# Layer 0's last five pairs of row tiles turned in 32x32 blocks by VectorE and moved through DRAM instead of transposed by TensorE

## The chip, the cores and the metric

The kernel runs on one NeuronCore of one Trainium2 chip. A core has a matrix engine (TensorE, PE in the profile, with PEld for its weight loads), a vector engine (VectorE, DVE), an engine for activation functions and copies (ScalarE, ACT), a general one (GpSimd, POOL) and a queue engine (SyncE, SP); the engines run side by side, each through its own instructions in order, and wait for one another by semaphores. Matrix results land in PSUM, everything else lies in SBUF, and transfers to and from DRAM are done by 16 DMA engines, started here by SP and by ACT. The metric is the device time of one execution in microseconds (us); lower is better.

## The reference, cut to what matters

There are N = 4096 nodes with D = 512 features and a dense 4096 x 4096 array `adj`. Layer 0 is attention inside 32 graphs of 128 nodes each, where the softmax's denominator runs over the whole row of `adj`; layer 1 is a graph attention with 8 heads over the mask `adj > 0`.

```python
h = jnp.maximum(_layernorm(x, axis=-1), 0.0)
# layer 0: attention within each graph of 128 nodes
query, key, value = h @ Wq.T + bq, h @ Wk.T + bk, h @ Wv.T + bv
a = jnp.where(mask, query @ key.T * scale, 0.0)
scores = (a + adj + adj) * jnp.where(mask, 1.0, -1000000.0)
x = x + (jax.nn.softmax(scores, axis=-1) * mask) @ value
# layer 1: 8 heads, one mask
h = jnp.maximum(_layernorm(x, axis=-1), 0.0)
mx = jnp.einsum('nf,hfd->hnd', h, W)
logits = s_i[:, :, None] + t_j[:, None, :]
attn = jax.nn.softmax(jnp.where(adj[None] > 0, logits, neg_inf), axis=-1)
x = x + einsum('hij,hjd->hid', attn, mx), heads side by side
```

## The kernel before, in words

**Tiles.** The 4096 rows are 32 row tiles of 128 (`NT`), one for each graph. Layer 0 takes two at a time: 16 pairs (`NG`, pair g is tiles 2g and 2g+1). A row of `adj` is read in two halves of 2048 columns (`load_adj`, 1 MB each, 7 buffers in turn), so a pair needs four.

**Stages.** A start (`fold`, up to about 42 us) multiplies the query and key weights into one matrix `m_sb` and works out what the biases add: `bk`, `bq` and a column `u_col` are spread into rows, `spread_bias` (L187) and L231, by matmuls of a broadcast column with the identity. Then comes layer 0's loop over g (42 to 335 us), then the last pair (to 349), then layer 1's projection for the tiles that are not yet projected (to 434), and layer 1's aggregation over the mask (`product`, L318 to L322, to the end).

**The loop over pairs.** Everything is written out by hand there (`tc.manual_schedule` for all five engines): each engine does its instructions in the order in which the program names them. In iteration g the names stand in this order:

- `load_pair(g + 2)` fetches the input rows of the pair two ahead into `xg`.
- `scores` (L578) multiplies this pair's queries gT with hT; VectorE adds twice the diagonal block of `adj` (L583), ScalarE takes the exponent.
- `queries` (L504) makes gT of pair g+1 in four PSUM groups, copied by ScalarE (L508). Between the groups, `mask_half` (VectorE, L144) writes the 8-bit mask of two row tiles of `adj` and `sum_half` (ScalarE, L547) sums the exponents of the same half; its elementwise output goes to `junk`, which nobody reads. `store_mask` writes the mask to `a_d` (L556), and `sum_half` starts the next `load_adj` into the half that it has done with (L110).
- `turned` transposes the attention weights (L601).
- `moments` and `normed0` (L117 to L129) normalise pair g+2: VectorE's statistics, GpSimd's inverse root, VectorE's normalisation.
- In iterations 7, 8, 9, 10 and 13, `prepare` (L271) projects a tile for layer 1 on PE.
- `values` (L517) makes v of pair g+1, `attend` (L609, L612) multiplies weights with v and adds the input; the sum x1 is stored to DRAM by ScalarE's queue (L615, `x_d<-x` in the profile). The row of tile g is fetched back (`fetch`, L439).
- `row_terms` (L491) is a dot product of each row of pair g+2 with `u_sb`.
- `turn` (L415) turns one tile of layer 1's normalised input in 32x32 blocks on VectorE; every four tiles `store` writes them to DRAM, and `move` (four transfers, L426 to L428) reads them back so that the whole is transposed: block (q, a) lands at (a, q).
- `turned0` transposes pair g+2 on PE: `relu_T`, four 128x128 transposes for a tile (L135), and one ScalarE relu from PSUM to `hT` (L136).

PSUM has four buffers `pp` for queries, projections, values and attend, used in turn. In layer 1's projection loop, the tile that is `far` = 10 tiles ahead decides when `move` is started: at `far % BY == 1`, with BY = 4.

The rule for the single transfer is that the place in the order decides: SP issues its transfers in the program's order, and one that has to wait holds those behind it.

Of the kernel before, what the change touches and what calls it, by code (L numbers as in the profile page):

```python
# [9 lines left out]
F32 = mybir.dt.float32  # L10
# [10 lines left out]
P = 128  # L21
N = 4096
D = 512
# [20 lines left out]
AB = 7  # L44
AHEAD = 10
# [8 lines left out]
def kernel(  # L54
# [33 lines left out]
    hT_d = dram.tile([NW, P, P // B, KC * P], F32, name="hT_d")  # L88
    x1_d = dram.tile([NT, P, D], F32, name="x1_d")
# [84 lines left out]
    def fold(sb, tmp, work, ps_t, ps_p, loads, between):  # L174
# [9 lines left out]
        def spread_bias(b):  # L184
            pp = ps_p.tile([P, D], F32, name="pp")
            for k in range(KC):
                nc.tensor.matmul(  # L187
                    pp[:, ts(k, P)], b[:, k : k + 1].to_broadcast([P, P]), ident,
                    start=True, stop=True,
                )  # L190
            row = work.tile([P, D], F32, name="b_row", tag="hn")
            nc.scalar.copy(row, pp)
            return row
# [33 lines left out]
        for m in range(KC):  # L227
            if m == 2:
                pp = ps_p.tile([P, D], F32, name="pp")
                for k in range(KC):  # L230
                    nc.tensor.matmul(  # L231
                        pp[:, ts(k, P)], u_col[:, k : k + 1].to_broadcast([P, P]), ident,
                        start=True, stop=True,
                    )
                nc.scalar.copy(u_sb, pp)
                pp = ps_p.tile([P, D], F32, name="pp")
                nc.tensor.matmul(pp[:, :1], zp.to_broadcast([P, P]), one, start=True, stop=True)
                nc.scalar.copy(z_sb, pp[:, :1])
            between(m, 0)
            pp = ps_p.tile([P, D], F32, name="pp")  # L240
            for k in range(KC):
                nc.tensor.matmul(  # L242
                    pp, wq[:, k, ts(m, P)], wk[:, k, :], start=(k == 0), stop=(k == KC - 1)
                )
            between(m, 1)
            nc.scalar.mul(m_sb[:, m, :], pp, SCALE)
# [140 lines left out]
    with ExitStack() as straight:  # L387
# [4 lines left out]
        with ExitStack() as prep:  # L392
# [71 lines left out]
            with (  # L464
# [20 lines left out]

                def row_terms(hns):

                    r = sb.tile([P, G], F32, name="r", bufs=3)
# [25 lines left out]
                def values(hT, t, later=False):  # L514
# [5 lines left out]
                    v = sb.tile([P, D], F32, name="v", bufs=4)  # L520
# [12 lines left out]
                def sum_half(i, h, diag, sums, counts):  # L533
# [9 lines left out]
                    for c0, c1 in pieces:  # L543
                        if c0 < c1:
                            n = counts[-1]
                            junk = sb.tile([P, NH], BF16, name="junk", bufs=1)
                            nc.scalar.activation(  # L547
                                junk[:, c0:c1], a[:, c0:c1], AF.Exp, scale=2.0 * NEG,
# [49 lines left out]
                def turned(s):  # L598
# [3 lines left out]
                    sT = sb.tile([P, G, P], F32, name="sT", bufs=1)  # L602
# [14 lines left out]
                def load_pair(g):  # L617
                    xg[g] = sb.tile([P, G, D], F32, name="xg", bufs=3)
# [44 lines left out]
                )  # L663
                for g in range(NG - 1):
                    new = G * (g + 1)
                    mine = g - 1
                    if g + 2 < NG:
                        load_pair(g + 2)
                    if g in (5, 9, 13):
                        store(g // BY - 1)  # L670
# [3 lines left out]
                    if g == NG - 2:  # L674
# [3 lines left out]
                        more = sb.tile([P, G, D], F32, name="xg", bufs=3)  # L678
# [19 lines left out]
                    s = scores(hT, gT, rs[g], *look)  # L698
                    ngT = queries(nhT, between)
                    sT = turned(s)  # L700
                    if g + 2 < NG:
                        ofs = [moments(xg[g + 2][:, t, :]) for t in range(G)]
# [10 lines left out]
                    if g + 2 < NG:  # L713
                        hns = normed0(g + 2, ofs)
# [12 lines left out]
                    if g + 2 < NG:  # L727
                        rs[g + 2] = row_terms(hns)
# [8 lines left out]
                    if g + 2 < NG:  # L737
                        nhT, hns = turned0(g + 2, hns)

# [37 lines left out]
            with by_hand:  # L777
# [6 lines left out]
                for i in range(LO, NT):  # L784
# [3 lines left out]
                    if far % BY == 1 and LO + AHEAD < far <= NT + 1:  # L788
# [414 lines left out]
```

## Time and profile before

| what | value |
|---|---|
| time, median of 3 runs | 931.07 us (929.63 to 931.77) |
| profiled execution | 930.15 us, span 928.3 us |
| TensorE busy | 919.4 us, 99% of the span |
| VectorE busy | 474.3 us, 51% |
| ScalarE busy | 261.1 us, 28% |
| GpSimd busy | 160.8 us, 17% |
| moved by DMA | 165.01 MB, mean 178 GB/s |
| `a<-adj`, issue to landing, median | 8.4 us for 1 MB |
| `mw<-a_d`, the same | 3.9 us for 128 KB |
| `x_d<-x`, the same | 7.3 us for 256 KB |

The page gives for each engine its busy time and its share of the span. A group of instructions is shown as line, engine, operation, output<-input, shape and count, then busy time and mean duration of one, then the idle time of the engine just before them and what ended it. Matmuls overlap in the array, so that a mean duration is longer than what one more of them costs; the chain of waits, which gives the time that a run of them took, shows the cost. The 40 slices show that the transfers are dense in the first third, where layer 0 reads `adj`, and thin afterwards:

```profile
DMA  8999999999899766762212122222222131313111
GB/s 333 415 333 390 366 372 377 345 368 352 309 350 370 238 203 182 208 154 57 69 52 85 55 83 61 76 69 68 82 56 83 55 91 46 91 46 92 46 46 37
```

A slice is 23.2 us. Layer 0's iterations start at 41.65 and then every 18.4 us, or every 21.9 where `prepare` is in them; iterations 9 to 14 start at 215.07, 236.95, 258.83, 277.20, 295.58 and 317.46.

### The profile page before, as it was taken

The numbers are of one execution on the slowest core, as the hardware profiler recorded it, in microseconds if no ns is written. First come the engines' busy times: TensorE is split into PE (matmuls) and PEld (weight loads), VectorE is DVE, ScalarE is ACT, GpSimd is POOL, SyncE is SP. The second block draws the span as 40 slices with busy tenths as digits, with TensorE's granted clock in tenths as the row PEclk, the third lists the DMA queues.
The fourth block names the chain that finished last, engine by engine and source line by source line (L and its number), as shares of the span: only waits on it lengthen the run. The fifth ranks groups of instructions, "written<-read, shape, count | busy, mean of one in ns | idle before, by whom it ended". The sixth has DMA issues, their size and how long they took to land.

```text
span 928.3 us, 13021 instructions
## 1 busy us (share of the span) xinstructions
PE 919.4 (99%) x4933; PEld 803.4 (87%) x4933; DVE 474.3 (51%) x1016; ACT 261.1 (28%) x507; POOL 160.8 (17%) x344
## 2 busy tenths in 40 slices
PE   9999999999999999999999999999999999999997
PEld 6776676767767778889999999999999999999997
DVE  4577987677778776736272424232333323242412
ACT  5477667655566653321000000000000000000000
POOL 1112111132211225644010101010101010101010
PEclk9999999999999999999999999999999999999999
DMA  8999999999899766762212122222222131313111
GB/s 333 415 333 390 366 372 377 345 368 352 309 350 370 238 203 182 208 154 57 69 52 85 55 83 61 76 69 68 82 56 83 55 91 46 91 46 92 46 46 37
DMA packets 63941, 165.01 MB, mean 178 GB/s; under 512 B 7042, under 2 KB 23810, under 8 KB 54658
## 3 DMA queue, kind: packets, MB, share of 16 engines
q1 hardware_dynamic: 54370, 147.35, 47.4%
q10 hardware_dynamic: 9504, 16.78, 4.8%
q8 instruction: 40, 0.66, 0.3%
q14 instruction: 27, 0.22, 0.1%
HBM read 122.16 MB, written 41.94 MB: 177 GB/s over the span
## 4 chain that ended last, share of the span: by engine, by line
PE 90%; DMA 6%; DVE 1%; ACT 1%; POOL 1%; issue 0%; SPq 0%; DVEq 0%; ACTq 0%
PE pg L322 52%; PE pp L517 10%; PE pp L504 10%; PE pp L271 9%; PE pss L578 3%; PE pp L609 3%; DMA xg<-x 2%; PE pp L242 1%; DMA row<-x_d 1%; PE pt L135 1%; DMA x_d<-x 1%; PE pl L322 1%; DMA a<-adj 1%; DMA hT_d<-blocks 0%; DMA bk_sb<-bk 0%
## 5 line engine op out<-in xcount | busy, mean ns | idle before, releaser
L322 PE MATMUL pg<-part,ata 128*128 128x348 f32 (+1 forms) x1536 | 246.8, 321 | 0.0
L322 PEld LDWEIGHTS pg<-part,ata 128*128 128x128 f32 x1536 | 244.5, 188 | 0.1
L322 PE MATMUL pg<-part,atb 128*128 128x348 f32 x1472 | 236.8, 322 | 0.0
L322 PEld LDWEIGHTS pg<-part,atb 128*128 128x128 f32 x1472 | 234.6, 189 | 0.1
L336 ACT COPY tot<-pg 128x522 f32<-128x522 f32 x31 | 18.5, 597 | 454.0 <-PE pg L322 454.0
L547 ACT ACTIVATE junk<-a 128x2048 bf16<-128x2048 f32 (+15 forms) x92 | 124.5, 1353 | 1.3
L517 PE MATMUL pp<-wv,hT 128*128 128x512 f32 x256 | 114.9, 592 | 0.0
L308 DVE CAST atb<-at 128x4096 fp32r<-128x4096 fp8e4 x16 | 36.7, 2295 | 152.6 <-PE pg L322 152.6
L271 PE MATMUL pp<-w1x,hT 128*128 128x256 f32 (+1 forms) x512 | 114.1, 383 | 0.3 <-DVE e L280 0.3
L504 PE MATMUL pp<-hT,m_sb 128*128 128x256 f32 x512 | 113.2, 379 | 0.0
L271 PEld LDWEIGHTS pp<-w1x,hT 128*128 128x128 f32 x512 | 96.7, 190 | 16.2 <-issue 1.9
L308 DVE CAST ata<-at 128x4096 fp32r<-128x4096 fp8e4 (+1 forms) x17 | 36.9, 2168 | 140.5 <-PE pg L322 140.4
L504 PEld LDWEIGHTS pp<-hT,m_sb 128*128 128x128 f32 x512 | 96.2, 190 | 12.8 <-issue 0.5
L517 PEld LDWEIGHTS pp<-wv,hT 128*128 128x128 f32 x256 | 47.9, 190 | 54.3 <-issue 53.5
L144 DVE TENSOR_SCALAR a<-a 128x512 fp8e4<-128x512 f32 x256 | 90.4, 447 | 1.3 <-DMA a<-adj 1.3
L854 POOL COPY den_all<-tot 128x1 f32<-128x1 f32 x31 | 5.7, 184 | 365.9 <-DVE tot L337 365.9
L858 POOL TENSOR_TENSOR tot<-tot,row 128x512 f32<-128x512 f32 x31 | 39.9, 1287 | 61.9 <-DVE tot L342 59.9
L121 POOL TENSOR_SCALAR ve<-mv 128x1 f32<-128x1 f32 x64 | 15.1, 236 | 190.4 <-DVE mv L119 190.3
L255 POOL TENSOR_TENSOR part<-e,part 128x522 fp32r<-128x522 f32 x32 | 40.7, 1271 | 12.8 <-ACT part L252 12.8
L123 POOL TENSOR_TENSOR rstd<-ve,neghalf 128x1 f32<-128x1 f32 x64 | 41.1, 642 | 5.3
L299 DVE STREAM_TRANSPOSE at<-mw 128x1024 f32<-128x1024 f32 x32 | 39.6, 1237 | 0.0
L280 DVE TENSOR_TENSOR e<-pp,e 128x256 f32<-128x256 f32 x64 | 25.1, 411 | 27.0 <-PE pp L271 13.7
(114 smaller groups left out, 658.4 us busy)
## 6 DMA issues: line engine op xcount, KB each, us to landing
a<-adj SPq DMA_DIRECT2D x64, 1024.0 KB, 8.4
a_d<-a SPq DMA_DIRECT2D x32, 512.0 KB, 9.0
mw<-a_d SPq DMA_DIRECT2D x128, 128.0 KB, 3.9
row<-x_d SPq DMA_DIRECT2D x60, 256.0 KB, 3.7
xg<-x SPq DMA_DIRECT2D x16, 512.0 KB, 10.7
x_d<-x ACTq DMA_DIRECT2D x32, 256.0 KB, 7.3
hT_d<-blocks SPq DMA_DIRECT2D x8, 1024.0 KB, 4.8
hT<-hT_d SPq DMA_DIRECT2D x32, 256.0 KB, 6.2
```

The source lines that it names most:

```text
L123: nc.gpsimd.tensor_tensor(rstd, ve, neghalf, ALU.pow)
L144: nc.vector.tensor_scalar(a8v[:, u], av[:, u], 0.0, None, ALU.is_gt, saturate=False)
L255: nc.gpsimd.tensor_sub(dst[:, :, 1, :], e3, dst[:, :, 0, :].bitcast(F32))
L271: nc.tensor.matmul(pm[g][:, :n], hT[:, k, :], w1x[:, k, g * HW : g * HW + n], start=(k == 0), stop=(k == KC - 1),)
L299: nc.vector.transpose(at8.rearrange("p c n b -> p (c n b)").bitcast(F32).rearrange("p (c u n) -> p c u n", c=NW, n=B), mw.rearrange("p u ( ...
L308: nc.vector.tensor_copy(at[:, c0 * BY : c1 * BY].rearrange("p (c b) q -> p c b q", b=BY), at8[:, c0:c1].rearrange("p c q b -> p c b q"),)
L322: nc.tensor.matmul(pg[:, : 2 * CW1].rearrange("p (s w) -> p s w", s=2)[:, :, :n], at[:, j, :], part(j)[:, c, :, :n], start=(j == 0), stop= ...
L504: nc.tensor.matmul(pp[:, : G * P], m_sb[:, k, ts(m, P)], hT[:, k, :], start=(k == 0), stop=(k == KC - 1),)
L517: nc.tensor.matmul(pp, hT[:, k, ts(t, P)], wv[:, k, :], start=(k == 0), stop=(k == KC - 1))
L547: nc.scalar.activation(junk[:, c0:c1], a[:, c0:c1], AF.Exp, scale=2.0 * NEG, accum_out=sums[:, n : n + 1],)
L578: nc.tensor.matmul(pss[:, t, :], gT[:, k, ts(t, P)], hT[:, k, ts(t, P)], start=(k == 0), stop=(k == KC - 1),)
L858: nc.gpsimd.tensor_add(num, num, row)
```

## The change

Pairs 11 to 15 of layer 0 (`BLOCKS = 11`) are no longer transposed by TensorE. `turn0` turns a normalised pair in 32x32 blocks on VectorE into a buffer `b0`; `store0` writes it to DRAM (`h0_d`, one transfer of 512 KB on SP's queue); `move0` reads it back with the blocks in transposed places (four transfers of 128 KB, into the same single buffer `b0`); `relu0` is two ScalarE instructions that apply the relu and write `hT`. This takes an iteration longer than a transpose on PE, so the pair is normalised an iteration earlier: n is g+2 for pairs below 11 and g+3 from then on. Pair 11 has no iteration of its own for that: it is normalised at the end of iteration 8 (`mhns`), and its `turn0`, `store0` and `row_terms` stand right after the scores of iteration 9. `load_pair` is an iteration earlier from g=6, which loads two pairs.

To hold this, `xg` and `r` have four buffers and `v` has three; `junk` is gone, its exponents being written over `a` itself, and `sT` shares the buffer of `s`.

Two smaller edits: the biases are spread by `nc.tensor.transpose` instead of a matmul with the identity, and in layer 1's projection loop `move` is started at `far % BY == 2`, one row tile later.

The diff:

```diff
--- before.py
+++ after.py
@@ -42,6 +42,7 @@
 SCALE = float(D) ** -0.5
 BIG_T = 40.0
 AB = 7
+BLOCKS = 11
 AHEAD = 10
 WARM = 10
 LO = 8
@@ -86,6 +87,7 @@
 
     a_d = dram.tile([NT, P, N // BY], F32, name="a_d")
     hT_d = dram.tile([NW, P, P // B, KC * P], F32, name="hT_d")
+    h0_d = dram.tile([NT // G, P, P // B, KC * G * B], F32, name="h0_d")
     x1_d = dram.tile([NT, P, D], F32, name="x1_d")
 
     ident = const.tile([P, P], F32, name="ident")
@@ -184,10 +186,7 @@
         def spread_bias(b):
             pp = ps_p.tile([P, D], F32, name="pp")
             for k in range(KC):
-                nc.tensor.matmul(
-                    pp[:, ts(k, P)], b[:, k : k + 1].to_broadcast([P, P]), ident,
-                    start=True, stop=True,
-                )
+                nc.tensor.transpose(pp[:, ts(k, P)], b[:, k : k + 1].to_broadcast([P, P]), ident)
             row = work.tile([P, D], F32, name="b_row", tag="hn")
             nc.scalar.copy(row, pp)
             return row
@@ -228,9 +227,8 @@
             if m == 2:
                 pp = ps_p.tile([P, D], F32, name="pp")
                 for k in range(KC):
-                    nc.tensor.matmul(
-                        pp[:, ts(k, P)], u_col[:, k : k + 1].to_broadcast([P, P]), ident,
-                        start=True, stop=True,
+                    nc.tensor.transpose(
+                        pp[:, ts(k, P)], u_col[:, k : k + 1].to_broadcast([P, P]), ident
                     )
                 nc.scalar.copy(u_sb, pp)
                 pp = ps_p.tile([P, D], F32, name="pp")
@@ -483,9 +481,39 @@
                         relu_T(ps_t, hn, hT[:, :, ts(t, P)])
                     return hT, hns
 
+                def turn0(hns):
+
+                    b0 = sb.tile([P, P // B, KC, G, B], F32, name="b0", bufs=1)
+                    for t, hn in enumerate(hns):
+                        nc.vector.transpose(
+                            b0[:, :, :, t], hn.rearrange("p (k q f) -> p q k f", k=KC, f=B)
+                        )
+                    return b0
+
+                def store0(g, b0):
+                    nc.sync.dma_start(h0_d[g], b0.rearrange("p q k t r -> p q (k t r)"))
+
+                def move0(g):
+                    b0 = sb.tile([P, P // B, KC, G, B], F32, name="b0", bufs=1)
+                    for q in range(P // B):
+                        nc.sync.dma_start(
+                            b0[ts(q, B)].rearrange("p a k t r -> p a (k t r)"),
+                            h0_d[g, :, q].rearrange("(a f) w -> f a w", f=B),
+                        )
+                    return b0
+
+                def relu0(b0):
+                    hT = sb.tile([P, KC, G * P], F32, name="hT")
+                    for t in range(G):
+                        nc.scalar.activation(
+                            hT[:, :, ts(t, P)].rearrange("p k (a r) -> p a k r", r=B),
+                            b0[:, :, :, t], AF.Relu,
+                        )
+                    return hT
+
                 def row_terms(hns):
 
-                    r = sb.tile([P, G], F32, name="r", bufs=3)
+                    r = sb.tile([P, G], F32, name="r", bufs=4)
                     for t, hn in enumerate(hns):
                         hu = sb.tile([P, D], BF16, name="hu", bufs=1)
                         nc.vector.scalar_tensor_tensor(
@@ -517,7 +545,7 @@
                         nc.tensor.matmul(
                             pp, hT[:, k, ts(t, P)], wv[:, k, :], start=(k == 0), stop=(k == KC - 1)
                         )
-                    v = sb.tile([P, D], F32, name="v", bufs=4)
+                    v = sb.tile([P, D], F32, name="v", bufs=3)
 
                     def biased():
                         nc.vector.tensor_add(v, pp, bv_sb)
@@ -543,9 +571,8 @@
                     for c0, c1 in pieces:
                         if c0 < c1:
                             n = counts[-1]
-                            junk = sb.tile([P, NH], BF16, name="junk", bufs=1)
                             nc.scalar.activation(
-                                junk[:, c0:c1], a[:, c0:c1], AF.Exp, scale=2.0 * NEG,
+                                a[:, c0:c1], a[:, c0:c1], AF.Exp, scale=2.0 * NEG,
                                 accum_out=sums[:, n : n + 1],
                             )
                             counts[-1] += 1
@@ -599,7 +626,7 @@
                     ps = ps_s.tile([P, G, P], F32, name="pss")
                     for t in range(G):
                         nc.tensor.transpose(ps[:, t, :], s[:, t, :], ident)
-                    sT = sb.tile([P, G, P], F32, name="sT", bufs=1)
+                    sT = sb.tile([P, G, P], F32, name="s", bufs=1)
                     nc.scalar.copy(sT, ps)
                     return sT
 
@@ -615,7 +642,7 @@
                     nc.scalar.dma_start(x1_d[i], x1)
 
                 def load_pair(g):
-                    xg[g] = sb.tile([P, G, D], F32, name="xg", bufs=3)
+                    xg[g] = sb.tile([P, G, D], F32, name="xg", bufs=4)
                     nc.sync.dma_start(
                         xg[g], x[g * G * P : (g + 1) * G * P, :].rearrange("(t p) d -> p t d", p=P)
                     )
@@ -661,11 +688,19 @@
                 by_hand.enter_context(
                     tc.manual_schedule(engines={E.PE, E.DVE, E.Activation, E.Pool, E.SP})
                 )
+                b0 = mhns = None
                 for g in range(NG - 1):
                     new = G * (g + 1)
                     mine = g - 1
-                    if g + 2 < NG:
+
+                    n = g + 2 if g + 2 < BLOCKS else g + 3 if g + 3 < NG else None
+                    if g + 5 <= BLOCKS:
                         load_pair(g + 2)
+                    if g + 5 >= BLOCKS and g + 3 < NG:
+                        load_pair(g + 3)
+                    if b0 is not None and g + 2 > BLOCKS:
+                        store0(g + 2, b0)
+                        b0 = None
                     if g in (5, 9, 13):
                         store(g // BY - 1)
                     if g == 1:
@@ -675,7 +710,7 @@
 
                         for i in (g, g + 1):
                             fetch(i, sb.tile([P, D], F32, name="hn"))
-                        more = sb.tile([P, G, D], F32, name="xg", bufs=3)
+                        more = sb.tile([P, G, D], F32, name="xg", bufs=4)
                         for t in range(G):
                             fetch(g + 2 + t, more[:, t, :])
                     if g in (6, 11, 14):
@@ -696,10 +731,16 @@
                             mask_half(new + 1, m - 2)
 
                     s = scores(hT, gT, rs[g], *look)
+                    if mhns:
+                        store0(g + 2, turn0(mhns))
+                        rs[g + 2] = row_terms(mhns)
+                        mhns = None
                     ngT = queries(nhT, between)
                     sT = turned(s)
-                    if g + 2 < NG:
-                        ofs = [moments(xg[g + 2][:, t, :]) for t in range(G)]
+                    if n:
+                        ofs = [moments(xg[n][:, t, :]) for t in range(G)]
+                    if BLOCKS <= g + 2 < NG:
+                        moved = move0(g + 2)
                     look_on(1, 0)
                     rest = prepare() if g in (7, 8, 9, 10, 13) else None
                     look_on(1, 1)
@@ -710,8 +751,8 @@
                         fetch(g)
                     if g == NG - 2:
                         of[g], of[g + 1] = moments(rows[g]), moments(rows[g + 1])
-                    if g + 2 < NG:
-                        hns = normed0(g + 2, ofs)
+                    if n:
+                        hns = normed0(n, ofs)
                     if 2 <= g < 2 + KC:
                         dots(g - 2)
                     v0 = values(nhT, 0, later=True)
@@ -724,8 +765,8 @@
                         of[0] = moments(rows[0])
                     if g:
                         relu1(mine)
-                    if g + 2 < NG:
-                        rs[g + 2] = row_terms(hns)
+                    if n:
+                        rs[n] = row_terms(hns)
                     if g == NG - 2:
                         relu1(g)
                         relu1(g + 1)
@@ -734,8 +775,14 @@
                     for i in (g, g + 1) if g == NG - 2 else (mine,) if g else ():
                         turn(i, rows[i], keep)
                     hT, gT, vs, look = nhT, ngT, nvs, nlook
-                    if g + 2 < NG:
+                    if g + 2 < BLOCKS:
                         nhT, hns = turned0(g + 2, hns)
+                    elif g + 2 < NG:
+                        nhT = relu0(moved)
+                    if n and n >= BLOCKS:
+                        b0 = turn0(hns)
+                    if g + 3 == BLOCKS:
+                        mhns = normed0(BLOCKS)
 
 
                 g = NG - 1
@@ -785,7 +832,7 @@
                     far = i + AHEAD
                     if far + 2 >= ahead:
                         load(far + 2)
-                    if far % BY == 1 and LO + AHEAD < far <= NT + 1:
+                    if far % BY == 2 and LO + AHEAD < far <= NT + 2:
                         move(far // BY - 1)
                     if far == NT + 1:
```

## The prediction, made before the changed kernel had run

> **What bounds the kernel now.** I read the busy list first, then PE's waits, PE's groups, and then the loop stage alone: its transfers, VectorE's order and the sync queue.
>
> ```profile
> PE 919.4 (99%) x4933; PEld 803.4 (87%) x4933; DVE 474.3 (51%) x1016; ACT 261.1 (28%) x507; POOL 160.8 (17%) x344
> ```
>
> TensorE is the bound, in every stage: of a span of 928.3 us it is idle 9. So work taken from it shows in full, and so does any wait that it is given. Its waits, all of them:
>
> ```profile
> PE pt L198 <- POOL ident masks.py:199: 1.5, 1, 1.5
> PE pp L609 <- DVE e L280: 0.8, 1, 0.8
> PE pt L205 <- DMA wkT_sb<-wkT: 0.4, 1, 0.4
> PE pp L271 <- DVE e L280: 0.3, 1, 0.3
> PE pt L205 <- ACT w L206: 0.2, 1, 0.2
> ```
>
> The reader is to see that only 1.1 us of wait is there to be won in the loop (both at g=7, whose iteration lasts 22.93 us against 21.88 of the others with a `prepare`). The work that the change takes from PE, from its groups and the chain:
>
> ```profile
> L135 PE MATMUL pt<-ident,hn 128*128 128x128 f32 x128 | 16.6, 273 | 0.0
> L187 PE MATMUL pp<-ident,bq_sb 128*128 128x128 f32 x8 | 1.2, 275 | 0.0
> L231 PE MATMUL pp<-ident,u_col 128*128 128x128 f32 x8 | 1.1, 275 | 0.0
> ```
>
> ```profile
> 18.31 0.89 PE pp L231 x8
> 258.12 0.87 PE pt L135 x8
> ```
>
> Instructions overlap: a mean of 273 ns in the group, but eight in 0.87 us on the chain, so 0.109 each is what one costs. A spread is four matmuls of two passes, 0.22 each.
>
> The second resource is the transfers. In windows from late in iteration 10 to late in 13 (columns: PE, PEld, DVE, ACT, POOL busy, clock, DMA share, GB/s):
>
> ```profile
> 252.00:271.00 19.00, 19.00 (x81) 13.01 (x80) 14.77 (x39) 10.98 (x21) 3.82 (x10) 1.00 1.02 346
> 271.00:289.00 18.00, 18.00 (x78) 12.48 (x77) 14.80 (x39) 12.20 (x25) 2.87 (x9) 1.00 0.98 357
> 289.00:311.00 22.00, 22.00 (x95) 15.71 (x94) 15.55 (x41) 15.08 (x30) 4.96 (x13) 1.00 0.99 379
> ```
>
> They are full just where the change adds transfers. VectorE has some 4 us free in 18. Its order at the head of an iteration (this is g=10, which starts at 236.95), and then the sync queue in g=11, which starts at 258.83:
>
> ```profile
> 238.94 0.42 DVE L583 SCALAR_TENSOR_TENSOR s<-diag,pss 128x256 f32<-128x256 f32 x1 [1.35 <-PE pss L578]
> 239.28 2.80 DVE L144 TENSOR_SCALAR a<-a 128x512 fp8e4<-128x512 f32 x8
> ```
>
> ```profile
> 273.07 0.43 SPq L556 DMA_DIRECT2D a_d<-a  x1
> 280.09 0.33 SPq L439 DMA_DIRECT2D row<-x_d  x1
> ```
>
> The queue stood still from 273.5 to 280.09, with nothing of its own to wait for but a store by ScalarE (`x_d<-x`, issued 273.02, landed 280.07). The waits on the queue say it too (15.9 us for three row fetches). In the program's order each transfer, of either queue, waits until the one eight places ahead has landed; a sync transfer eight places after a ScalarE store inherits its latency.
>
> **What the Trainium skill says.** "DMA: Bandwidth & Descriptors", section "Issuing engines are not separate DMA queues": transfers of both issuing engines run on the same 16 DMA engines and interleave. The trace agrees (an `adj` half takes 8.4 us in the median, 4.9 at best). Same page, "Two DMAs through the same engine are not ordered": reading what another transfer wrote needs the wait on its completion; so `move0` must wait for `store0`. "VectorE: DVE Perf Modes", "The three transpose paths": VectorE turns 32x32 blocks, not a whole 128x128; hence the DRAM trip. The trace has such a turn (L415, 0.70 us for 128x512). "TensorE: Matmul & The Clock Gate", "Part 4: PE-mode transpose": about 275 ns in a kernel's context; trace 273, but pipelined 0.109.
>
> **The change, part by part.**
>
> *Removed from PE.* Pairs 11 to 15: 5 x 0.87 = 4.36 us. Spreads: 12 passes x 0.11 = 1.3 us, but the start is then bound elsewhere: the exp of half (0,0), now in place, waits for the mask of that half (ends 21.3; exp began at 19.77), and it stands ahead of the last `m_sb` copy and hT on ScalarE, which the first values need; I work out 26.3 for these instead of 27.0: 0.7 (0.4 to 1.0). The waits of g=7 go, as pair 9 is loaded an iteration earlier: 1.05. Sum 6.1.
>
> *In-place exp.* In an ordinary iteration the mask ends 0.3 us before its exp starts, and an exp costs 1.90 us for 2048 elements whatever it writes to. Nothing. Buffers (`xg`, `r`, `v`, `sT`): their readers are an iteration ahead; hidden by PE's 18 us. Late `move` one tile later: hT4 landed 6 us or more before use, a tile is 3.5; nothing to 0.3.
>
> *VectorE.* A turn of a pair is 2 x 0.70 = 1.4 us in iterations 8 to 12, within the 4 us free.
>
> *g=8 and g=9.* At the end of g=8 pair 11's moments (2 x 0.86), about 1 us for POOL's rstd, and 1.1 for norms are queued on VectorE; g=9's `s` comes after them at about S+5.3 (S the start of scores; 2.0 before). Then turn0 (1.4) and row_terms (1.4) stand ahead of the mask of half (new,0): it ends at about S+9.8 instead of 3.8. Queued behind: on ScalarE the in-place exp of that half, then gT1, gT2. PE needs gT1's PSUM buffer for the second half of `project1` and gT2's for values. Exp to 11.8, gT1 12.2, second exp, gT2 14.7; PE would want it at 12.4. Stall 2.3 (1.5 to 3).
>
> *g=11.* move0(13) is four transfers of 128 KB. Its second and third stand eight places behind the two x1 stores of the same iteration, issued at S+14.2 and 15.1. These same two stores landed at S+21.2 and 23.6 before (280.07, 282.43), with two `adj` halves issued just ahead of them; now the queue is held, and these halves come later. Between 2.0 us of latency (the least, at 313.28) and 8.5, I take landings at S+17.5 and 18.3, when what was issued by S+9 has drained. The nearest row for a part is `mw<-a_d`, same shape, 2.5 to 4.2 nearly idle. So the last part lands at S+20.2 at the earliest, likely about 21.4; relu0 adds 1.1 (two of L136's). Queries of g=12 want it at 17.5 + 1.8 = 19.3. Stall 2.0 to 6; I take 3.2.
>
> *g=12.* What the queue held back (two halves, mask words, row, pair, store0, two more halves, words, move0) is 7.6 MB between the last part of move0(13) and that of move0(14). At 365 GB/s: 20.8 us, against 17.5 of PE work. Stall 3.3 (0.5 to 5). g=10 has some 2.5 us to spare, and g=13, with its `prepare`, loses 0 to 1; I take 0.4.
>
> Stalls: 2.3 + 3.2 + 3.3 + 0.4 = 9.2. Net -6.1 + 9.2 = +3.1: 931.07 + 3.1 = 934.2.
>
> **The rivals.** *All hidden:* the b0 trip and VectorE's detour cost nothing. 931.07 - 6.1 = 925.0, faster. For it: ScalarE and VectorE are idle a third of these windows, and each transfer has an iteration. Against: full DMA windows, and the order of g=9. *Short stalls:* g=9's 2.3, g=11's minimum 2.0, g=12's 0.5: 931.07 - 6.1 + 4.8 = 929.8, about no change. For it: x1 stores did land in 2.0 us where the queue was empty. Against: 7.0 and 8.5 us at g=11, 5.7 and 6.3 at g=10. *DMA the bound:* stalls at their upper ends, 3 + 6 + 5 + 1 = 15: 940. For it: one late x1 store delays everything behind it in the queue. Against: the 128 KB parts are short and the windows after 311 run at 0.69.
>
> **How the numbers follow.** Likeliest, stalls of 7 to 13: 0.48, 934.2. Short stalls: 0.24. Hidden: 0.17. Bound by DMA: 0.11. Part of the short stalls and of the hidden case lies under 929.2: faster 0.26. The band 929.2 to 932.9 takes the rest of the short ones and the low edge of the likeliest: 0.22. Slower 0.52. For eight in ten I leave half of the hidden case and the tail above 939 out: 926.5 to 939.
>
> **What would show it.** Right: PE waits of about 2 us at values or `project1` in g=9 on gT or exp; at queries of g=12 and 13 on relu0 behind b0's transfers; `h0_d` parts issued at the landing of x1 stores; x1 lasting over 5 us; L135 at 88 instructions. Wrong: no PE wait over 1 us in iterations 9 to 14 (then 925), or parts of move0 landing within S+17. If PE's waits sum to under 6 us I have mis-sized the transfers; if the spreads give less than 0.4 us, the start.

## The result, and the profile after

The changed kernel took 943.99 us in the median of 5 (939.19 to 945.27) against 930.85 for the kernel before (5 runs, 929.63 to 931.77): ratio 1.0126, interval 1.0098 to 1.0154. It is slower by some 12 us. The forecast was slower too, but 934.2, with eight chances in ten for 926.5 to 939.

The profiled execution took 939.2, the shortest of the five, with a span of 937.4 us. Its busy list:

```profile
PE 916.7 (98%) x4881; PEld 799.7 (85%) x4881; DVE 481.8 (51%) x1026; ACT 257.1 (27%) x507; POOL 161.7 (17%) x344
```

TensorE's waits (total, times, longest):

```profile
PE pp L532 <- ACT hT L508: 10.3, 2, 9.5
PE pt L197 <- POOL ident masks.py:199: 1.5, 1, 1.5
PE pp L269 <- ACT gT L536: 1.3, 1, 1.3
...
PE pp L545 <- ACT gT L536: 0.3, 1, 0.3
```

And the group of its transposes:

```profile
L137 PE MATMUL pt<-ident,hn 128*128 128x128 f32 x88 | 11.4, 273 | 0.0
```

TensorE has 40 transposes less, as meant, but one wait of 9.5 us at the queries of g=12 (S = 276.26), for `relu0`. S is the start of an iteration's `scores`, as in the prediction; g=11 starts at 258.76 here. The chain of waits (start, duration, what) shows what held `relu0` up:

```profile
255.46 7.33 DMA x_d<-x
262.80 0.33 SPq L437
...
263.23 6.17 DMA xg<-x
269.42 0.71 DVE stats L119
...
273.48 1.41 DVE x L639 x2
274.91 8.29 DMA x_d<-x
283.22 0.30 SPq L499
...
283.57 2.82 DMA b<-h_d
...
286.55 1.16 ACT hT L508 x2
...
287.75 9.69 PE pp L532 x32
```

Read from the bottom: the queries wait for relu0, relu0 for the last part of the read-back (`b<-h_d`), that part for the queue (L499 is move0), the queue for an x1 store (`x_d<-x`) of g=11. And this is the second such link: the stores of g=10 had held the row fetch (L437), and with it the load of the next pair and `store0`, in the same way. The late load held VectorE's statistics in turn, so that the x1 stores of g=11 were issued at S+15.5 and 16.2 instead of the 14.2 and 15.1 of before. The sync queue over that stretch:

```profile
262.80 0.33 SPq L437 DMA_DIRECT2D row<-x_d  x1
263.23 0.41 SPq L646 DMA_DIRECT2D xg<-x  x1
265.77 0.33 SPq L494 DMA_DIRECT2D h_d<-b  x1
266.18 2.39 SPq L426 DMA_DIRECT2D hT<-hT_d  x4
269.46 1.75 SPq L112 DMA_DIRECT2D a<-adj  x2
271.93 0.34 SPq L583 DMA_DIRECT2D a_d<-a  x1
273.08 10.92 SPq L499 DMA_DIRECT2D b<-h_d  x4
```

The four parts of move0 take 10.9 us to issue (parts at 273.08, 281.38, 283.22 and 283.57 by their records). The trip of pair 13, from store0's issue at 265.77 to the last landing at 286.39, is 20.6 us; those of pairs 11, 12, 14 and 15 are 17.8, 15.4, 17.2 and 16.5. Pair 13's began 7.0 us into its iteration, of 17.5 us without a transpose.

The windows of the wait and after it (PE, PEld, DVE, ACT, POOL busy, clock, DMA share, GB/s):

```profile
276.00:288.00 12.00, 2.46 (x18) 2.03 (x18) 2.18 (x5) 1.15 (x2) 0.53 (x2) 0.78 0.83 305
288.00:306.00 18.00, 18.00 (x54) 11.67 (x55) 14.51 (x39) 11.28 (x22) 3.16 (x9) 0.86 1.03 373
```

All engines nearly stand still in the first window (TensorE is busy for 2.46 us of 12), the DMA engines do not (0.83). And the clock is down: the 32 query matmuls took 9.69 us on the chain instead of 6.91.

Where the time went, from the starts of `scores` in the two traces: start -0.5; g=7 -1.05; five iterations shorter by 0.87 each, -4.4; g=9 +2.2; g=10 +1.05; g=12 +12.3 (9.5 of wait, 2.8 of clock); g=14 +0.1; from g=15 to the end -0.6. Sum +9.1, as the spans (928.3, 937.4).

### The profile page after: what moved, and what is told of

Its sections match the earlier page's. It is cut to its first block, busy times and chain, and to the rows that moved or that the text cites. A ratio compares the mean times of both kernels' runs of the same rounds, so it can differ in the third digit from the quotient of the medians.

```text
span 937.4 us, 12943 instructions
## 1 busy us (share of the span) xinstructions
PE 916.7 (98%) x4881; PEld 799.7 (85%) x4881; DVE 481.8 (51%) x1026; ACT 257.1 (27%) x507; POOL 161.7 (17%) x344
## 4 chain that ended last, share of the span: by engine, by line
PE 92%; DMA 4%; DVE 1%; ACT 1%; issue 0%; POOL 0%; SPq 0%; ACTq 0%
PE pg L320 51%; PE pp L269 12%; PE pp L532 11%; PE pp L545 10%; PE pp L636 2%; PE pss L605 2%; DMA x_d<-x 2%; PE pp L240 1%; DMA b<-h_d 1%; PE pl L320 1%; PE pt L137 1%; DMA xg<-x 1%; DMA a<-adj 1%; DMA bk_sb<-bk 0%; PE pss L628 0%
## 5 line engine op out<-in xcount | busy, mean ns | idle before, releaser
L532 PE MATMUL pp<-hT,m_sb 128*128 128x256 f32 x512 | 116.0, 385 | 10.3 <-ACT hT L508 10.3
L574 ACT ACTIVATE a<-a 128x2048 f32<-128x2048 f32 (+15 forms) x92 | 123.8, 1352 | 4.8 <-DVE a L146 4.4
```

What stands on the lines that cost most here:

```text
L532: nc.tensor.matmul(pp[:, : G * P], m_sb[:, k, ts(m, P)], hT[:, k, :], start=(k == 0), stop=(k == KC - 1),)
L574: nc.scalar.activation(a[:, c0:c1], a[:, c0:c1], AF.Exp, scale=2.0 * NEG, accum_out=sums[:, n : n + 1],)
```

## The experiments

Ratios are to the kernel before on the same chip, where its median was 930.4 to 931.4.

**1. Is it the order on the queue?** The ring of the texts below is the eight completion semaphores that the transfers of SP and ScalarE take in turn (100 to 107 in the trace): one that takes a semaphore waits until its last user has landed. Transfers issued by GpSimd carry others (111 to 118). Three kernels take move0 out of the way of the x1 stores: by naming it earlier, with in one of them pair 11's moments earlier too, or by taking the stores off the ring. The early place:

```diff
+                    if BLOCKS <= g + 2 < NG:
+                        moved = move0(g + 2)
                     ngT = queries(nhT, between)
                     sT = turned(s)
                     if n:
                         ofs = [moments(xg[n][:, t, :]) for t in range(G)]
-                    if BLOCKS <= g + 2 < NG:
-                        moved = move0(g + 2)
```

> The changed kernel with move0 named right after the scores, ahead of the iteration's first two adj halves. Theory A (ring of eight: in g=11 the second and third part of move0 wait for the two x1 stores of the same iteration, which land 7 to 8 us after issue): the parts now stand eight places behind the pair's load, store0 and two hT parts instead, so they go out as soon as store0 has landed; TensorE's wait at the queries of g=12 falls from 9.5 us to at most 2, the clock stays at 1.00, and the time is 926 to 931 us. Theory B (the DMA engines are full in g=11, the extra transfers are late in whatever order): the wait stays at 6 us or more and the time at 938 or more. Theory C (the single buffer b0 and VectorE waiting for it): no change of the wait at g=12, 939 to 944.

Pair 11's moments too:

```diff
                         hns = normed0(n, ofs)
+                    if g + 3 == BLOCKS:
+                        mofs = [moments(xg[BLOCKS][:, t, :]) for t in range(G)]
...
-                        mhns = normed0(BLOCKS)
+                        mhns = normed0(BLOCKS, mofs)
```

> As the run with the early move0, and besides the moments of pair 11 are named in the middle of g=8, right after the normalisation of pair 10, instead of at its end. If the wait of 1.3 + 0.3 us in g=9 (project1 and values, on gT) comes from the two rounds of statistics and inverse root at the end of g=8, the scores' sum s in g=9 comes at about S+2.5 instead of 5.2, the mask of the first half ends about 3 us earlier and the wait goes: about 1.6 us less than the run with the early move0 alone. If it comes from turn0 and row_terms before the masks, it stays.

The stores off the ring, with `move0` in its old place:

```diff
-                    nc.scalar.dma_start(x1_d[i], x1)
+                    nc.gpsimd.dma_start(x1_d[i], x1)
```

> The changed kernel with x1 stored by GpSimd's queue, whose transfers count on semaphores of their own, and nothing else altered. Theory A (ring of eight shared with the x1 stores): no part of move0 waits for an x1 store any more; the four parts of g=11 go out within 2 us of one another and land by about S+21; the wait at g=12 falls to 0 to 3 us; 927 to 933 us. Theory B (engines full): wait 6 us or more, 938 us or more. GpSimd's own cost of starting a transfer can add a little at the inverse roots.

Measured, in this order: 941.43 us (ratio 1.0119, interval 1.0082 to 1.0157), 939.74 (1.0089, 1.0070 to 1.0107) and 940.65 (1.0110, 1.0088 to 1.0132). Theory A in its pure form falls. With x1 on semaphores of its own the parts of g=11 went out at 271.3 to 274.9, evenly, and yet landed at 284.0 to 285.7, 11 to 13 us later; the wait was 7.8 us instead of 9.5. With the early place the last of them landed at 279.0 and the wait at g=12 was 2.95, but one of 7.1 came at g=13. Its chain:

```profile
275.87 4.18 DMA x_d<-x
280.13 0.35 SPq L112
280.54 0.42 SPq L583
281.06 0.61 SPq L112
281.84 0.43 SPq L112
282.32 0.48 SPq L583
282.84 0.45 SPq L437
283.39 14.11 DMA xg<-x
```

The held queue let four `adj` halves and two mask stores go at once; the pair's load behind them took 14.1 us, and store0 of pair 14, issued at 284.67, landed at about 298.8. So the wait had only moved. With the moments earlier too it was in two parts, 5.5 us at g=12 and 3.9 at g=13.

The part on g=9 held. VectorE after the change, and with the moments named earlier:

```profile
218.78 0.41 DVE L610 SCALAR_TENSOR_TENSOR s<-diag,pss 128x256 f32<-128x256 f32 x1
219.11 1.30 DVE L488 STREAM_TRANSPOSE b<-hn 128x512 f32<-128x512 f32 x2
```

```profile
215.54 0.42 DVE L610 SCALAR_TENSOR_TENSOR s<-diag,pss 128x256 f32<-128x256 f32 x1 [0.47 <-PE pss L605]
215.88 1.30 DVE L488 STREAM_TRANSPOSE b<-hn 128x512 f32<-128x512 f32 x2
```

`s` comes 3.2 us earlier and g=9 lasts 21.01 us instead of 23.16. So it was enough to take the statistics and the inverse root from the end of g=8; turn0 and row_terms before the masks cost nothing by themselves. Whether taking these away instead would have been enough too was not run.

**2. The trip left out, in halves, or with nobody waiting.**

```diff
-                        store0(g + 2, b0)
+                        moved = b0
...
-                        moved = move0(g + 2)
```

> The changed kernel without the trip through DRAM: store0 and move0 are left out, and relu0 reads the buffer as turn0 left it, so the 32x32 blocks stay in their own places and the output of the pairs 11 to 15 is not the reference's. All of VectorE's and ScalarE's new work stays (turn0, the order in g=9, relu0, the single buffer b0, exponents in place). Theory B (the added transfers meet full DMA engines): no wait of TensorE over 0.5 us in g=10 to 14, the wait in g=9 of 1.6 us stays, and the time is before - 4.4 (transposes) - 0.5 (start) - 1.0 (g=7) - 0.6 (after the loop) + 1.6 = 925.5 us. Theory C (VectorE's and ScalarE's order, b0's single buffer): waits of 6 us or more stay, 936 or more.

Then with store0 put back; and with all transfers, move0 going to another DRAM array (of that diff only the new destination is shown):

```diff
                         moved = b0
+                        store0(g + 2, b0)
```

> As the run without the trip, but with store0 (half of the added bytes, 512 KB a pair, which nobody waits for but the next turn0); move0 is left out and relu0 reads the buffer as turned, so the output of those pairs is not the reference's. Theory B in its simple form (bytes alone: what is added delays the adj halves): some wait returns, 1 to 4 us in all, 927 to 930 us. If the loss lies in somebody waiting for move0 at the end of a full queue and not in the bytes, it is as the run without the trip, within 0.5 us.

```diff
-                            b0[ts(q, B)].rearrange("p a k t r -> p a (k t r)"),
+                            h1_d[g, ts(q, B)],
```

> All the transfers of the changed kernel, in their places on the sync queue, but nobody on an engine waits for the read-back: move0 copies the same pieces of h0_d to another DRAM array, and relu0 reads the buffer as turned, so the output of the pairs 11 to 15 is not the reference's. If the added bytes and the held queue slow the adj halves and so the engines (theory B by bytes): waits of 5 us or more at g=11 to 13, 934 us or more. If the loss is that TensorE waits for the end of the trip itself (store0 at the end of a full queue, then the read-back at the end of it again): no wait over 1.3 us outside g=9, 926 to 929 us.

Without the trip: 926.52 (0.9960, 0.9946 to 0.9974). PE's waits are the small ones of g=9 and the start:

```profile
PE pp L269 <- ACT gT L536: 1.3, 1, 1.3
...
PE pp L545 <- ACT gT L536: 0.3, 1, 0.3
...
PE pp L532 <- ACT hT L508: 0.3, 1, 0.3
```

So all of VectorE's and ScalarE's new work is hidden but for g=9, and the trip costs 12 to 17 us (941.28 and 943.99 in two sets of the changed kernel: 15 and 17 by the medians, 12 and 15 by the ratios). Theory C falls as a cause of its own. With the trip, though, the single buffer does make VectorE wait for the read-back's reader:

```profile
DVE b L488 <- ACT hT L508: 11.0, 2, 9.8
```

A second buffer for `b0` was not run. With store0 alone: 927.04 (0.9967, 0.9955 to 0.9980), within 0.6 us of the run without; half of the bytes, at the head of the iteration, delay nobody. With all the transfers but no engine waiting for the read-back: 940.32 (1.0099, 1.0081 to 1.0117), the first of the two alternatives, but not by the `adj` halves. TensorE waited 10.5 us at g=13 behind VectorE, which stood here:

```profile
DVE stats L120 <- DMA xg<-x: 19.2, 3, 11.8
```

move0's parts went out between 274.71 and 285.09, two of them at the landing of x1 stores; what stood behind them in the queue was the load of the next pair, issued at 288.46, 13 us into its iteration. VectorE does its work in order, so everything behind those statistics waited. So a loss of this size needs nobody who waits for the read-back: the queue that it holds is enough. (The copy goes from DRAM to DRAM here, so its transfers are not quite those of the changed kernel.)

**3. The added bytes taken away elsewhere.** The two mask stores of an iteration are as many bytes as a trip.

```diff
                 def store_mask(i):
+                    if 20 <= i < 30:
+                        return
```

> The changed kernel, whole trip and all orders, but without the ten mask stores of iterations 9 to 13 (tiles 20 to 29, 512 KB each, on the same sync queue): exactly the 1 MB an iteration that the trip adds is taken from the same engines and the same queue. Layer 1 reads the words of tile 19 in their place, so its output for these tiles is not the reference's. If the DMA engines being full is the cause: the waits at the queries of g=12 and 13 fall to under 2 us in sum, the 1.6 us of g=9 stay, 926 to 929 us. If the trip is too long in itself (two transfers one after the other, the ring of eight, the single buffer): 5 us of wait or more stay, 934 us or more.

The same with x1 on GpSimd's queue, and with the early place of move0, as the diffs under 1:

> As the run without ten mask stores, and x1 stored by GpSimd's queue on semaphores of its own (layer 1 reads tile 19's words for the tiles 20 to 29, so that part of the output is not the reference's). Without the mask stores the last two parts of move0 in g=11 still waited for the x1 stores (issued 280.10 and 280.80, the stores' landings, against 280.6 for the landing of the second part), and 5.5 us of wait stayed at the queries of g=12. If bytes and ring together are the whole cause: at most 2.5 us of wait there and 927 to 931 us, the sum being more than the runs with one remedy alone (934.35 and 940.65). If the trip is too long even so: 933 or more.

> As the run without ten mask stores, and move0 named right after the scores (layer 1 reads tile 19's words for the tiles 20 to 29). The read-back then stands ahead of two adj halves and clear of the x1 stores. With full engines alone, the early place only moved the wait from g=12 to g=13 (store0 of pair 14 landed 14 us after issue). With 1 MB an iteration less: no wait over 1.5 us outside g=9 and 926.5 to 929 us. If a wait of 3 us or more stays at g=12 or 13, the held queue's bursts of adj halves are a cause of their own.

Measured: 934.35 (1.0034, 1.0022 to 1.0046), 935.27 (1.0041, 1.0020 to 1.0061) and 932.18 (1.0012, 1.0002 to 1.0021). The first wins back 5 to 10 us, about half of the trip's cost, but not all: 934.35 is where its second alternative had begun. In it, the chain before the queries of g=12 still runs through an x1 store and the last part of the read-back:

```profile
274.84 5.94 DMA x_d<-x
...
280.80 2.59 DMA b<-h_d
```

It left 5.5 us of wait; with x1 on its own semaphores the wait was 2.9 in the profiled execution of 931.88, but the median was no better. With the early place, store0 of pair 14 took 13.6 us behind a burst of adj halves, and 4.8 us of wait came at g=13. So about half of the cost goes with the mask stores. That these are bytes alone is not shown: a mask store that is left out also leaves its place on the queue and in the ring. The other half stays; the two traces show store0 and the read-back each at the end of a queue that is held or has just been let go, but no run parts this from the rest.

**4. The trip on GpSimd's queue.**

```diff
-                    nc.sync.dma_start(h0_d[g], b0.rearrange("p q k t r -> p q (k t r)"))
+                    nc.gpsimd.dma_start(h0_d[g], b0.rearrange("p q k t r -> p q (k t r)"))
...
-                        nc.sync.dma_start(
+                        nc.gpsimd.dma_start(
                             b0[ts(q, B)].rearrange("p a k t r -> p a (k t r)"),
```

> The changed kernel with store0 and move0 on GpSimd's queue, which has rings and semaphores of its own, and pair 11's moments named in the middle of g=8. The trip no longer stands behind adj halves in the same queue and holds none back. If the place in the queue decides, the trip takes under 15 us in all from g=10 on and the waits at the queries fall to under 3 us in sum: 926 to 930 us. If the DMA engines being full decides whatever the queue, each half of the trip takes 8 us or more and waits of 5 us or more stay: 934 us or more.

946.39 (1.0166, 1.0148 to 1.0184), worse than all. The trip no longer held the sync queue, and still store0 took 4 to 10 us and each part of the read-back 6.5 to 11; PE waited 4.8, 5.3 and 5.8 us at g=10, 12 and 13. Time and waits are those of the second alternative, but the run does not prove its reason, the full engines: GpSimd, too, does its work in order, and `move0` stood behind the inverse roots of the next pair there. In g=9 store0 had landed at 222.16 and the read-back was issued at 227.04; that gap is 3.8 to 4.9 us for three of the five pairs and 0.6 and 0.7 for the others. GpSimd's queue with the early place was not run.

**5. Fewer pairs, later.** `BLOCKS` was set to 14, 15 and 16, with the loads one ahead from g=6 as before (`ONE`) and the moments of the first moved pair named early.

```diff
-BLOCKS = 11
+BLOCKS = 14
+ONE = 11
...
-                    if g + 5 <= BLOCKS:
+                    if g + 5 <= ONE:
...
-                    if g + 5 >= BLOCKS and g + 3 < NG:
+                    if g + 5 >= ONE and g + 3 < NG:
```

> The changed kernel with only the pairs 14 and 15 turned by VectorE (BLOCKS = 14), the pairs still loaded one ahead from g=6, and pair 14's moments named in the middle of g=11. Their trips fall in g=12 and g=13, where layer 0 has loaded nearly all of adj. Theory B: hardly any wait, 2 x 0.87 + 0.5 + 1.0 + 0.6 = 3.8 us less than before, 927 us. Theory A (ring of eight) and C (order of VectorE): a wait of 2 us or more remains at the queries of g=13 or 14, 929 us or more.

> Only the pairs 14 and 15 by VectorE, loads one ahead from g=6, pair 14's moments in the middle of g=11, and move0 named right after the scores, ahead of the first two adj halves of its iteration. Without the early place the read-back of pair 14 stood behind two adj halves and landed at 299.35, 4.5 us too late. Now store0 lands at about 286 and the four parts 3 us later; no wait at g=13: 926 to 928 us. If the burst of adj halves behind the held queue delays store0 of pair 15 as it did with pair 14 when all five pairs were moved: a wait at the queries of g=14 and 930 or more.

> As the run with only the pairs 14 and 15 by VectorE, but with store0 and move0 on GpSimd's queue instead of the early place. If the queue decides: no wait at the queries of g=13, 926 to 928 us. If not: a wait of 3 to 6 us there, 931 to 935 us.

> As the kernel with the pairs 14 and 15 by VectorE and the early read-back, but pair 15 alone (BLOCKS = 15): its whole trip falls in g=13. One pair's transposes are 0.87 us, so 928.1 us if the trip is hidden and no order costs; more if store0 and the read-back, both in one iteration, take over 20 us together.

> The changed kernel with no pair turned by VectorE at all (BLOCKS = 16): what is left are the exponents in place, pairs loaded one ahead from g=6, the spreads by transposition and the late move. Expected: 0.5 (start) + 1.0 (g=7) + 0.6 (after the loop) less than before, 929.0 us. If loading one ahead or the exponents in place cost something where the transfers are dense, TensorE shows a wait in g=9 to 12 and the time is 930 or more.

| pairs by VectorE, place of move0 | us | ratio (interval) |
|---|---|---|
| 14, 15, after the moments | 934.73 | 1.0046 (1.0028 to 1.0064) |
| 14, 15, GpSimd's queue | 936.42 | 1.0074 (1.0047 to 1.0101) |
| 14, 15, right after scores | 929.86 | 0.9983 (0.9969 to 0.9997) |
| 15 alone, right after scores | 928.10 | 0.9965 (0.9951 to 0.9978) |
| none | 928.32 | 0.9967 (0.9955 to 0.9979) |

I had thought g=12 free of load, but the DMA share was 0.91 there (276 to 294): in the first kernel the read-back landed at 299.35, behind two adj halves issued 1 to 3 us ahead of it, and the queries of g=13 waited 5.6 us. On GpSimd's queue they waited 8.1. Here the early place did help: the profiled execution of that kernel, 928.36, has no wait at the queries. But a trip that is hidden earns at most its 0.87 us a pair: pair 15 alone is no faster than none, and the median of two pairs with the early place, 929.86, is no better than that of none; its longer executions were not profiled. The kernel with no pair turned by VectorE, which keeps the rest of the change, beats both kernels, the one before by 0.3% and the changed one by over 1%. Its PE waits only at the start:

```profile
PE pt L198 <- POOL ident masks.py:199: 1.5, 1, 1.5
PE pt L205 <- ACT w L206: 0.7, 1, 0.7
PE pt L205 <- DMA wkT_sb<-wkT: 0.3, 1, 0.3
```

**6. The small edits alone, and the changed kernel again.**

The first two are single hunks of the change, put on the kernel before: the two `transpose` hunks, and this one.

```diff
-                    if far % BY == 1 and LO + AHEAD < far <= NT + 1:
+                    if far % BY == 2 and LO + AHEAD < far <= NT + 2:
```

> The kernel before with only the biases spread by transposition. My count of passes: 12 passes less of 0.11 us, and the exponents still go to their own buffer and wait for no mask: layer 0's loop starts 1.3 us earlier than before (41.65), at 40.3, and the time is 929.7. If ScalarE's copies bound the start, the loop starts at 41.1 to 41.65 and the gain is 0 to 0.6 us.

> The kernel before with only the late move, at far % BY == 2. If the 0.6 us by which the changed kernel is shorter from the scores of g=15 to the end (592.7 against 593.3) come from it, the same stretch is 592.7 here and the time 930.0 or 0.4 to 0.6 us less than before; if not, 593.3 and no change.

> The changed kernel unaltered, to see a second execution in the profile: the profiled one took 939.2 us, the median is 944. If the extra 5 us are a longer wait of the same kind, the profile of a longer execution shows the wait at the queries of g=12 above 9.5 us or a further one at g=13, and the clock below 1.00 for longer; if they lie elsewhere, a stretch outside iterations 9 to 14 is longer.

The spreads: 929.65 (0.9990, 0.9982 to 0.9998), loop from 41.33 instead of 41.65. Only the spread of `u_col` counts, 0.44 us; the two others stand ahead of a wait for the weights' transfers and ScalarE's copies. In-place exponents were not what bound the start: ScalarE waited 1.55 us for the mask there and the values began at 26.53, against 26.69 with the spreads alone. The late move: 930.05 (0.9995, 0.9986 to 1.0003), no change that can be told, though from the scores of g=15 to the end it took 592.6 us, near the changed kernel's 592.7, against 593.3 before.

The changed kernel again: 941.28 (1.0093, 1.0061 to 1.0125; 6 runs, 939.6 to 949.2), profiled at 945.8. PE's wait:

```profile
PE pp L532 <- ACT hT L508: 14.0, 3, 9.1
```

Two links of its chain:

```profile
230.73 11.39 DMA b<-h_d
...
280.50 8.31 DMA x_d<-x
```

The wait of g=12 is the same (9.1), and g=10 has one more, of 4.6 us, as the last part of pair 11's read-back took 11.4 us instead of 7.9. With the lower clock after each wait this is the whole difference from the shorter execution; what makes one execution's transfers later than another's is open.

## Why the prediction was wrong

- **Bound, transposes, g=7**: right. 40 transposes fewer, 0.87 us a pair, 1.05 at g=7.
- **Start**: 0.7 forecast, 0.5 measured; wrong on its cause (two of the three spreads hidden, in-place exponents not the bound), so the near hit is luck.
- **g=9**: 2.3 forecast, 2.2 measured, at the places and by the queue of work on VectorE that were named.
- **g=11, the step that failed**: "landings at S+17.5 and 18.3", a last part at about 21.4, and so a stall of 3.2 at the queries of g=12. The stores landed at about S+22.6 and S+24.5, the last part at S+27.6, and the stall was 9.5. The path was the one named; the latencies on it were mis-sized. I had set every transfer of g=11 at its old place in the iteration and reasoned that a held queue leaves the engines emptier. But the queue was late already: the x1 stores of g=10 had held store0 to S+7.0, and hT, the adj halves and the words all went out just ahead of the stores. The old trace's 21.2 and 23.6, which I had and set aside, were nearer. Nor does the path explain the size: with the x1 stores off the ring the wait was still 7.8 us, as the parts themselves took 11 to 13 us to land, where I had reckoned with the 2.5 to 4.2 us of a nearly idle queue.
- **Clock**: 2.8 us at g=12, in no term of the sum; it was put at nothing without a reason. The Trainium skill ("TensorE: Matmul & The Clock Gate", "Why this matters for your kernels") warns of idle gaps over about 3 us, and my own stalls were at that mark.
- **g=10 and g=12 on**: 2.5 us to spare forecast at g=10, but 1.05 us lost in one execution and 7.2 in the other; 3.3 forecast for g=12's backlog, none measured in the profiled execution, where g=12 lasted 29.8 us instead of 17.5 and so left time for the trip of pair 14 (17.2). The backlog's 7.6 MB include the two x1 stores, which its list leaves out; what it lists is 7.1 MB.
- **The rival "all hidden"**, 925.0, is nearly what remains without the trip: 926.52, 4.1 below the kernel before there; the 2 us that are wanting are g=9's. The rest of the loss is the trip's, and it was under-sized: 12 to 17 us against 6.9 (3.2, 3.3 and 0.4).

## What to carry to other kernels

A round trip through DRAM inside a loop is two transfers one after the other, and here, where the DMA engines are full, each had the latency of full queues, not of idle ones. Take it from the old trace's own transfers in that very stretch (here 7 to 8.5 us for 256 KB; the trips took 15.4 to 20.6 us), add what the queue holds back, and compare with the time from the first issue to the first reader. In this loop, where the DMA engines ran at 0.98 to 1.02 already, none of the places and queues tried for all five trips was good; with the early places the wait moved to the next iteration. With 0.87 us to win for a pair and some 10 us to lose by one late trip (12.3 at g=12 of the change), such a change is best tried on one pair first, where the engines are least busy.

## What the runs showed of the hardware that was not expected

TensorE's clock after a wait. The 32 matmuls of `queries` take 7.07 us by the timeline without a wait before them (6.91 on the chain, which leaves out the overlap at the end). After waits of different lengths:

| wait before, us | 32 matmuls, us | run |
|---|---|---|
| 0.60 | 7.17 | without ten mask stores |
| 2.95 | 7.17 | early place |
| 2.92 | 8.80 | without mask stores, x1 on its own semaphores |
| 3.91 | 9.69 | early place and moments |
| 4.83 | 10.11 | without mask stores, early place |
| 5.26 | 8.57 | trip on GpSimd's queue |
| 5.61 | 9.91 | pairs 14 and 15, after the moments |
| 7.11 | 9.25 | early place |
| 8.11 | 8.61 | pairs 14 and 15, GpSimd's queue |
| 9.54 | 9.69 | the change |
| 10.51 | 9.44 | all transfers, nobody waiting for the read-back |

Beyond 3.9 us the wait's length doesn't matter: it costs 1.5 to 3.0 us more, without a trend. The trace's clock tells why. The granted clock falls to 0.50 during the wait and goes back to 1.00 in one step some microseconds after it. In the change it was 0.50 from 282.63 to 292.87, so the matmuls, which began again at 287.75, ran at half speed for 5.1 us and lost 2.6. After 8.11 us of wait they ran so for only 2.9 us (302.98 to 305.91). At 2.9 us of wait it went either way: in one run the clock fell at 280.92, 0.1 us before the matmuls began again, and stayed down for 3.4 us; in the other it stayed at 1.00. This agrees with the page cited above.
